# A four-layer convolution network: smaller pieces for the stores of the attention scores

## Chip, cores and metric

The kernel runs on one core of a Trainium2 chip. The metric is the time of one execution on the device in microseconds (us); the number for a kernel is the median of several executions. The profile is one more execution, recorded by the hardware profiler.

## What is computed

The input `x` has the shape (4, 256, 64, 64) in f32. Four layers follow each other, each of the form `x = x + layer(groupnorm(x))`. The change lies in layer 0, an axial attention over the columns of the image with 16 groups of channels:

```python
qkv = bn(einsum('nci,oc->noi', xp, w_qkv))         # n = 4*64, 64 positions i
q, k, v = split(qkv)                               # 16 groups, 8 + 8 + 16 channels
qe = einsum('ngci,cij->ngij', q, q_emb)
ke = einsum('ngci,cij->ngij', k, k_emb)
qk = einsum('ngki,ngkj->ngij', qe, ke)             # the scores
sim = softmax(bn(concat([qk, qe, ke])).sum(1))
attn, attn_e = einsum(sim, v), einsum(sim, v_emb)
```

The batch norm of `qk`, `qe` and `ke` needs sums over the whole batch, so all scores are computed and put away before the first softmax. Layers 1 to 3 are 3x3 convolutions with ternary, binary and generated weights.

## The kernel before

Layer 0 has three stages. The first normalises the input, projects it to q, k and v, and writes q and k to the scratch tensors `q_d[b]` in DRAM. The second computes the scores `qk`, writes them to `qk_d[b]` (one tensor for each of the 4 batch items, shape 8 x 128 x 4096), and gathers the sums for the batch norm; beside this it prepares the weights of the later layers. The third (`from_scores`) reads the scores back, forms the softmax and multiplies with the values. Then come the convolutions.

The second stage is a loop over 4 batch items `b` and 8 pairs of groups `gp`, 32 steps in all (L634, L635). A step has four beats, over `nb` and `jh` (L642, L645). In each beat:

- `projections` (L457) has SyncE load a piece of q and k for a later step, 128 KB with 64 rows of 2 KB (L463), pinned to its place in the program (L468). The data are needed two values of `j`, that is four steps, later.
- `position_terms` (L495) runs 64 small matmuls into PSUM (L505), and VectorE moves the result to SBUF in two transposes (L512).
- `finish(last, k)` (L612) calls `product` (L517) for the step before: 64 matmuls (L526), two ScalarE evictions into the tile `o` (L532) and a sum of squares (L538). So the tile `o` of a step is filled in the four beats of the next step.
- `finish` then issues one store out of the list `whole` (L616 to L625). A tile is put on `whole` after its fourth product, so its four stores are written in the beats of the step after that. Each store is pinned by `keep_in_program_order`.
- One slice of the weight preparation, mostly on VectorE, runs until the generator `weights` is used up.

The tile `o` (L640) has 128 partitions of 4096 f32 (16 KB), with two buffers. The first store of a tile needs all four products, so SyncE waits for ScalarE there; the other three have nothing new to wait for. The second buffer is free again when the four stores have landed, and is written by the first product of the step after next.

DRAM row `2 j + r` of `qk_d[b][gp]` belongs to partition `64 r + j`. A store before takes the partitions of one `r` and one half of the columns: 64 rows of 8 KB, 512 KB. The scores of the last step are stored after the loop in two pieces of 1 MB (L660), which the change leaves alone.

All loads and stores that matter here go through SyncE's queue, in program order: the loads of L463, the stores, at the end of the stage the loads of the tables `rw`, `ve` and `cnt` of the third stage (L771 to L779), the last scores (L660), the values `vb` (L820) and the scores `si` (L855). The tile framework gives every DMA of SyncE's and ScalarE's queues one of eight semaphores in turn, and a DMA waits until the one that had its semaphore before has landed. The POOL queue carries the prepared weights (L567, L596) and the loads of the raw ones (L574, L578).

Of the kernel before, what the change touches and what calls it, by code (L numbers as in the profile page):

```python
# [21 lines left out]
HW = 4096  # L22
# [19 lines left out]
def network(ctx: ExitStack, tc, x, wqkv, relm, relt, relw, relv, counts, masks, vecs, rowv, ab, w1, l2w1, l2w2, l3w, mats, out):  # L42
# [4 lines left out]
    nc = tc.nc  # L47
# [5 lines left out]
    def scratch(name, shape):  # L53
        return dram.tile(shape, F32, name=name, tag=name)
# [4 lines left out]
    qk_d = [scratch(f"qk_d{b}", [GP, P, HW]) for b in range(B)]  # L59
# [106 lines left out]
    with ExitStack() as ph:  # L166
# [112 lines left out]
        for b in range(B):  # L279
            xs, gm, rs = ready  # L280
            qs = [qp.tile([P, 8, 8, 64], F32, name=f"qs{t}_{b}", tag="qs") for t in range(2)]
            for k in range(NB):
# [37 lines left out]
                if k % 2 == 1:  # L320
                    for r in range(2):
                        nc.scalar.dma_start(
                            out=vt_d[b][k // 2, r].rearrange("p a c m -> p a (c m)"),
                            in_=vs.rearrange("p (a r c) m -> p r a (c m)", r=2, c=16)[:, r],
# [7 lines left out]
                if k in (3, 7) and 2 * b + k // 4 - 1 in range(len(pieces)):  # L332
                    i = 2 * b + k // 4 - 1
# [3 lines left out]
            for t in range(2):  # L337
                for l in range(8):
                    nc.sync.dma_start(
                        out=q_d[b][:, l, t].rearrange("a r c f -> (r c) a f"),  # L340
                        in_=qs[t][:, EIGHT[l]].rearrange("p a h -> p (a h)"),
# [36 lines left out]
        for t in range(2):  # L378
            for l in range(8):
                nc.gpsimd.dma_start(  # L380
                    out=qs_d[t, l].rearrange("r c a f -> (r c) a f"), in_=qtot[:, t, EIGHT[l]]
# [28 lines left out]
    with ExitStack() as ph:  # L410
# [106 lines left out]
        def product(units, o, k, col, gp, name):  # L517

            ps = [psq.tile([P, 8, 64], F32, name=f"pq_{name}_{k}_{nb}", tag="pq") for nb in range(2)]
            for m in range(8):  # L520
                n = 8 * k + m
                for nb, ts in enumerate(units):
                    for g in range(2):
                        src = 64 * (g ^ nb)
                        rows = slice(src, src + 64)
                        nc.tensor.matmul(  # L526
                            ps[nb][64 * g : 64 * g + 64, m, :], lhsT=ts[1][rows, n // 2, :, n % 2],
                            rhs=ts[0][rows, n // 2, :, n % 2], start=True, stop=True, tile_position=(src, 64 * g),
                        )
            for nb in range(2):  # L530
                n = 32 * nb + 8 * k
                nc.scalar.activation(  # L532
                    o[:, :, n : n + 8, :], ps[nb].rearrange("p n (a b) -> p a n b", b=2), AF.Copy,
                    accum_out=acc[:, nb, gp, col : col + 1],
                )
            part = o.rearrange("p a (x n) b -> p a x (n b)", x=2)[:, :, :, 16 * k : 16 * k + 16]
            junk = jp.tile([P, 32, 2, 16], BF16, name=f"sq_{name}_{k}", tag="sq", bufs=1)
            nc.scalar.activation(junk, part, AF.Square, accum_out=acc[:, 2, gp, col : col + 1])  # L538
# [73 lines left out]
        def finish(step, k):  # L612
            units, o, b, gp = step
            product(units, o, k, 4 * b + k, gp, f"{b}_{gp}")

            if whole:  # L616
                wb, wgp, wo, part = whole[0]
                store = nc.sync.dma_start(
                    out=qk_d[wb][wgp].rearrange("(j r) f -> r j f", r=2)[part % 2][:, bass.ts(part // 2, HW // 2)],
                    in_=wo[bass.ts(part % 2, 64), bass.ts(part // 2, 16)].rearrange("p a n b -> p (a n b)"),  # L620
                )
                tc.keep_in_program_order(store)
                whole[0] = (wb, wgp, wo, part + 1)
                if part == 3:
                    whole.pop()  # L625
            if k == 3:
                whole.append((b, gp, o, 0))
# [6 lines left out]
        for b in range(B):  # L634
            for gp in range(GP):  # L635
                j = 4 * b + gp // 2
                if j == 2 and gp % 2 == 0:
                    load_sums()
                q = qs[j]
                o = op.tile([P, 32, 64, 2], F32, name=f"o_{b}_{gp}", tag="o")  # L640
                units = []
                for nb in range(2):  # L642
                    ts = [tp_.tile([P, 16, 64, 2], F32, name=f"t{t}_{b}_{gp}_{nb}", tag=f"t{t}") for t in range(2)]
                    units.append(ts)
                    for jh in range(2):  # L645
                        if j + 2 < 4 * B:
                            projections(j + 2, 4 * (gp % 2) + 2 * nb + jh)
                        position_terms(q, ts, gp, nb, jh, f"{b}_{gp}_{nb}")
                        if last is not None:
                            finish(last, 2 * nb + jh)  # L650
                        if j > 0:
                            next(weights, None)
                last = (units, o, b, gp)
                term_sums(j, q, gp % 2)
                if gp % 2 == 0 and j + 1 < 4 * B:
                    scaled(j + 1, qs[j + 1])
        for k in range(4):
            finish(last, k)
        for r in range(2):
            nc.sync.dma_start(  # L660
                out=qk_d[B - 1][GP - 1].rearrange("(j r) f -> r j f", r=2)[r],
                in_=o[bass.ts(r, 64)].rearrange("p a n b -> p (a n b)"),
# [80 lines left out]
    def from_scores(general, keep):  # L743
# [373 lines left out]
        X_PLACES = [(0, 1, 2, 3), (4, 5, 0, 2), (1, 3, 4, 0), (5, 2, 1, 4)]  # L1117

        def conv_layer(name, ph, weights, layout, own, load, biases, first, finish):


# [768 lines left out]
```

## Time and profile before

| | us |
|---|---|
| median of 3 runs (2811.41 to 2813.65) | 2812.06 |
| the profiled execution | 2810.18 |
| its span, first to last instruction | 2808.3 |
| TensorE busy in the span | 2416.8 (86%) |
| VectorE busy | 1980.8 (71%) |
| ScalarE busy | 1204.5 (43%) |
| SyncE's DMA queue (q1): 195232 packets, 359.5 MB, share of the 16 DMA engines | 42.3% |

In a profile line, L12 is line 12 of the kernel. Engines are PE (TensorE matmul), PEld (TensorE weight load, beside PE), DVE (VectorE), ACT (ScalarE), POOL (GpSimd) and SPq (SyncE's queue, where a row is the issuing of a DMA, not its transfer). In a wait, `<-` names what ended it; "issue" is time in which an engine waited for nothing that the profile shows. The second stage lies at about 300 to 946 us of the span. 31 of its 32 tiles `o` are stored by L618, 124 stores; the 30 steps between the first stores of neighbouring tiles last 16.9 to 23.9 us, 19.7 us in the mean.

### The profile page before, as it was taken

Reading aid. Unit: us, or ns where it says so; the run is one execution under the profiler, and the core shown is the slowest. Engines: PE = TensorE matmul, PEld = TensorE weight load, DVE = VectorE, ACT = ScalarE, POOL = GpSimd, SP = SyncE. Lnnn points to the kernel's source line nnn. Section 1 sums busy time; section 2 is a strip of 40 time slices with the busy share of each in tenths; the row PEclk is TensorE's granted clock in tenths of the full one; section 3 lists DMA queues with packets and bytes.
Section 4 is the critical chain, followed back from the end, with each engine's and each line's share of the span. In section 5 each row is a group of like instructions: output and inputs, shape, how many; then the busy total and the mean of one; then the engine's idle time right before and its main releaser. Section 6 shows DMA issues by size and latency. Waiting matters only on the chain.

```text
span 2808.3 us, 77698 instructions
## 1 busy us (share of the span) xinstructions
PE 2416.8 (86%) x34632; PEld 1583.8 (56%) x34632; DVE 1980.8 (71%) x3362; ACT 1204.5 (43%) x1984; POOL 105.4 (4%) x201
## 2 busy tenths in 40 slices
PE   7999888888887778888874899998988859999998
PEld 4666555555555566667663677776555424444443
DVE  6665788878665455566657878986888877958642
ACT  4555355545444654454443564653448521110100
POOL 0000100000000100000000000000000000000000
PEclk9999899989999798989986899999999979999999
DMA  6867375657545777777766456534336752324101
GB/s 240 270 188 212 81 198 144 165 146 186 143 124 148 218 251 246 253 244 252 253 228 226 163 171 202 172 120 179 125 121 247 283 189 91 120 105 150 45 33 44
DMA packets 258233, 489.81 MB, mean 174 GB/s; under 512 B 26785, under 2 KB 143137, under 8 KB 237153
## 3 DMA queue, kind: packets, MB, share of 16 engines
q1 hardware_dynamic: 195232, 359.50, 42.3%
q0 software_dynamic: 14400, 66.53, 6.1%
q10 hardware_dynamic: 48256, 58.73, 6.1%
q8 instruction: 273, 4.47, 0.6%
q14 instruction: 72, 0.58, 0.1%
HBM read 281.46 MB, written 203.23 MB: 173 GB/s over the span
## 4 chain that ended last, share of the span: by engine, by line
issue 23%; PE 18%; DMA 10%; DVE 10%; ACT 5%; POOL 0%; SPq 0%; ACTq 0%; DVEq 0%; POOLq 0%
PE dc L1356 8%; DMA at_d<-o_False 3%; PE e_False L866 2%; DMA x<-x_d 2%; PE pr_False L935 2%; PE pc L1450 2%; DVE pt L876 2%; PE pe_False L969 2%; PE den_False L917 2%; DMA dx<-in_x 1%; DMA qc_False<-q_d 1%; ACT pt L906 1%; DVE e_tr L1439 1%; DMA z_d<-dx 1%; PE pa_False L944 1%
## 5 line engine op out<-in xcount | busy, mean ns | idle before, releaser
L1065 PE MATMUL gc<-gtr,g_u 128*128 128x512 f32 x1152 | 504.5, 600 | 11.1 <-DVE gtr L1043 6.7
L512 DVE STREAM_TRANSPOSE t<-pd 128x1024 f32<-128x1024 f32 x256 | 304.7, 1228 | 136.7 <-PE pd L505 131.9
L1065 PEld LDWEIGHTS gc<-gtr,g_u 128*128 128x128 f32 x1152 | 219.6, 191 | 287.6 <-issue 270.2
L505 PE MATMUL pd<-rm,qb 64*32 64x256 f32 x8192 | 322.6, 406 | 59.7 <-DVE t L512 30.3
L532 ACT ACTIVATE o<-pq 128x512 f32<-128x512 f32 x256 | 150.6, 594 | 311.6 <-PE pq L526 311.6
L1450 PE MATMUL pc<-e_tr,e_k 128*64 128x512 bf16 x2304 | 265.4, 391 | 18.3 <-DVE e_tr L1439 11.8
L1356 PE MATMUL dc<-dh,d_u 128*128 128x512 f32 x768 | 235.0, 416 | 35.8 <-ACT dh L1333 35.8
L505 PEld LDWEIGHTS pd<-rm,qb 64*32 64x32 f32 x8192 | 174.5, 112 | 160.1 <-issue 65.1
L906 ACT ACTIVATE pt<-pt,sm 128x512 f32<-128x512 f32 x256 | 162.6, 709 | 173.9 <-DVE pt L876 173.9
L1356 PE MATMUL dc<-dl,d_u 128*128 128x512 f32 x768 | 229.9, 409 | 0.3
L1450 PEld LDWEIGHTS <-e_k 128*64 128x64 bf16 x2304 | 146.7, 112 | 133.9 <-issue 26.9
L526 PEld LDWEIGHTS pq<-t,t 64*64 64x64 f32 x8192 | 146.3, 139 | 100.7 <-issue 89.1
L526 PE MATMUL pq<-t,t 64*64 64x64 f32 x8192 | 168.4, 227 | 40.1 <-issue 35.6
L1356 PEld LDWEIGHTS dc<-dh,d_u 128*128 128x128 f32 x768 | 149.5, 196 | 77.1 <-ACT dh L1333 37.7
L876 DVE TENSOR_TENSOR pt<-e_False,si_False 128x1024 f32<-128x1024 f32 x128 | 151.4, 1215 | 30.6 <-PE e_False L866 30.3
L1356 PEld LDWEIGHTS dc<-dl,d_u 128*128 128x128 f32 x768 | 146.4, 192 | 42.1 <-DVE dl L1334 3.6
L1083 ACT COPY gc_c<-gc 128x512 f32<-128x512 f32 x32 | 18.6, 581 | 344.8 <-PE gc L1065 344.8
L866 PE MATMUL e_False<-qc_False,rw 32*128 32x256 f32 x1024 | 129.7, 474 | 25.5 <-DVE pt L876 12.5
L538 ACT ACTIVATE sq<-o 128x1024 bf16<-128x1024 f32 x128 | 135.3, 1057 | 4.0
L293 PE MATMUL po<-xg,wt 128*128 128x512 f32 x256 | 120.2, 608 | 5.3 <-DVE st L300 3.7
L969 PE MATMUL pe_False<-pt,ve 128*32 128x64 f32 x4096 | 90.3, 243 | 35.6 <-issue 28.7
L308 PE MATMUL pv<-wt,xg 128*128 128x256 f32 x512 | 120.6, 384 | 0.0
(403 smaller groups left out, 3596.0 us busy)
## 6 DMA issues: line engine op xcount, KB each, us to landing
si_False<-qk_d SPq DMA_DIRECT2D x64, 1024.0 KB
qk_d<-o SPq DMA_DIRECT2D x124, 512.0 KB
x<-x_d SPq DMA_DIRECT2D x32, 1056.0 KB
xa<-in_x SPq DMA_DIRECT2D x16, 1024.0 KB
vt_d<-vs ACTq DMA_DIRECT2D x32, 512.0 KB
q_d<-qs SPq DMA_DIRECT2D x64, 256.0 KB
qb<-q_d SPq DMA_DIRECT2D x128, 128.0 KB
qc_False<-q_d SPq DMA_DIRECT2D x64, 256.0 KB
```

Of the source, the lines that this page charges most:

```text
L505: nc.tensor.matmul(pds[t][32 * c : 32 * c + 32, m].rearrange("p j k -> p (j k)"), lhsT=q[rows, 2 * (gp % 2) + g, a, 32 * nb : 32 * nb + 32 ...
L512: nc.vector.transpose(ts[t][:, :, 32 * jh : 32 * jh + 32].rearrange("p a j b -> p j a b"), pds[t].rearrange("p m j k -> p j m k"),)
L526: nc.tensor.matmul(ps[nb][64 * g : 64 * g + 64, m, :], lhsT=ts[1][rows, n // 2, :, n % 2], rhs=ts[0][rows, n // 2, :, n % 2], start=True, ...
L532: nc.scalar.activation(o[:, :, n : n + 8, :], ps[nb].rearrange("p n (a b) -> p a n b", b=2), AF.Copy, accum_out=acc[:, nb, gp, col : col + 1],
L538: nc.scalar.activation(junk, part, AF.Square, accum_out=acc[:, 2, gp, col : col + 1])
L866: nc.tensor.matmul(es[x_ // 2][:, x_ % 2, :, :, par], lhsT=rw[rows, 63 - i : 127 - i].rearrange("p j r -> p (j r)"), rhs=q[rows, :, par, k ...
L876: nc.vector.tensor_tensor(dst, e, src, ALU.add)
L906: nc.scalar.activation(s, s, AF.Exp, scale=s2q[:, gp : gp + 1])
L969: nc.tensor.matmul(ps[32 * a : 32 * a + 32, m // 2, :, m % 2], lhsT=ve[:, 63 - i, :], rhs=pt[:, i // 2, a, :, i % 2], start=True, stop=Tru ...
L1065: nc.tensor.matmul(ms[k], lhsT=u[t][:, dx, k, bass.ts(co, P)], rhs=vs[t][:, k, :, dx : dx + 64], start=(first and dx == 0), stop=(last and ...
L1356: nc.tensor.matmul(at[k], lhsT=u[t][:, dx, k, bass.ts(co, P)], rhs=v[:, k, :, dx : dx + 64], start=(first and p_ == 0 and dx == 0), stop=( ...
L1450: nc.tensor.matmul(m[64 * g : 64 * g + 64], lhsT=parts[:, g, i, k, dx, :], rhs=vs[g][:, k, 8 * (q % 2) : 8 * (q % 2) + 8, dx : dx + 64], s ...
```

## The change

Each store of 512 KB becomes four of 128 KB. In beat `part` (0 to 3) the pieces `i = 4 part` to `4 part + 3` are issued one behind the other: pieces with even `i` take partitions 0 to 63, those with odd `i` take 64 to 127, and `i // 2` picks one of eight column blocks of 512 f32. So a row of a piece is 2 KB, and a beat now stores a quarter of the columns of all 128 partitions, where it stored half the columns of half of them. A tile has 16 stores in place of 4, with the same bytes to the same places.

```diff
             if whole:
                 wb, wgp, wo, part = whole[0]
-                store = nc.sync.dma_start(
-                    out=qk_d[wb][wgp].rearrange("(j r) f -> r j f", r=2)[part % 2][:, bass.ts(part // 2, HW // 2)],
-                    in_=wo[bass.ts(part % 2, 64), bass.ts(part // 2, 16)].rearrange("p a n b -> p (a n b)"),
-                )
-                tc.keep_in_program_order(store)
+                for i in range(4 * part, 4 * part + 4):
+                    store = nc.sync.dma_start(
+                        out=qk_d[wb][wgp].rearrange("(j r) f -> r j f", r=2)[i % 2][:, bass.ts(i // 2, 512)],
+                        in_=wo[bass.ts(i % 2, 64), bass.ts(i // 2, 4)].rearrange("p a n b -> p (a n b)"),
+                    )
+                    tc.keep_in_program_order(store)
                 whole[0] = (wb, wgp, wo, part + 1)
                 if part == 3:
                     whole.pop()
```

## The prediction, on record before the result

> **What bounds the kernel now.** I read the page first, then the timeline of SyncE's queue in the second stage, then the waits there, and last the DMA share in and between the bursts of stores. The timeline shows two tiles of scores:
>
> ```profile
> 613.10 0.46 SPq L618 DMA_DIRECT2D qk_d<-o  x1
> 613.61 0.63 SPq L463 DMA_DIRECT2D qb<-q_d  x1
> 614.29 1.86 SPq L618 DMA_DIRECT2D qk_d<-o  x1
> 616.20 0.62 SPq L463 DMA_DIRECT2D qb<-q_d  x1
> 616.86 2.10 SPq L618 DMA_DIRECT2D qk_d<-o  x1
> 619.00 0.63 SPq L463 DMA_DIRECT2D qb<-q_d  x1
> 619.97 1.75 SPq L618 DMA_DIRECT2D qk_d<-o  x1
> 621.77 0.64 SPq L463 DMA_DIRECT2D qb<-q_d  x1
> 630.68 0.47 SPq L618 DMA_DIRECT2D qk_d<-o  x1
> ```
>
> The stores are written one to a beat, but they run as a burst: the first waits for the finished tile, the other three and the four loads between them follow at once. SyncE is busy from 613.1 to 622.4, 9.3 us, and idle until 630.7. The first store takes 0.46 us to issue, the later ones about 1.9 us: these are held back by the transfers ahead of them, not by the issuing. The waits say the same; columns are sum, count and longest, the first row from the queue's own waits, the others from the stage:
>
> ```profile
> SPq L618 <- ACT o L532: 337.1, 31, 28.4
> ...
> ACT o L532 <- PE pq L526: 284.2, 126, 6.3
> ...
> DVE t L512 <- PE pd L505: 128.7, 77, 6.7
> ...
> PE pq L526 <- issue: 35.0, 27, 3.6
> PE pd L505 <- DVE t L512: 28.8, 23, 2.2
> ...
> PE pd L505 <- issue: 26.9, 24, 2.8
> PE pq L526 <- ACT o L532: 4.3, 3, 2.9
> ```
>
> SyncE waits 337 us for tiles. ScalarE and VectorE wait for matmuls, TensorE for VectorE and for its own issue. In the whole stage no row has ScalarE waiting for a store to free its buffer, nor VectorE or TensorE for a load of q and k. TensorE, busy 83% to 86% in each window of 100 us, with VectorE at 62% to 84%, sets the pace. The stores are off the path. How far off, the next ScalarE rows and the DMA share tell (the windows are one burst and the rest of its step):
>
> ```profile
> 634.41 0.60 ACT L532 ACTIVATE o<-pq 128x512 f32<-128x512 f32 x1 [2.57 <-PE pq L526]
> ...
> 613.10:625.60 12.50, 11.08 (x397) 7.49 (x403) 12.26 (x23) 6.22 (x15) 0.56 (x1) 1.00 0.84 232
> 625.60:630.68 5.08, 4.39 (x134) 3.38 (x119) 3.15 (x4) 3.83 (x12) 0.53 (x1) 1.00 0.35 135
> ```
>
> The last two columns are the busy share of the 16 DMA engines and GB/s. The transfers of the burst end about 12.5 us after it starts. The buffer that they free is first written at 634.41, 21.3 us after the burst started. That leaves about 8 us of slack in each step.
>
> **What the Trainium skill says.** "SBUF — State Buffer", section "Door 1: The DMA port swizzle", says that the bandwidth depends on how many of 16 ports the partitions reach, and that partitions 0 to 63 and 64 to 127 lie on different ports; half the partitions reach half of them. The trace agrees: the 8 KB packets of L618, each from 64 partitions, take 613 ns in the median and 309 ns at best, which is 214 and 424 GB/s over 16 engines. "DMA: Bandwidth & Descriptors", section "Why small descriptors are slow", gives a packet a fixed overhead of about 3 cycles beside its 32-byte beats: estimated from that, 67 cycles for the 64 beats of 2 KB, some 5% over. In the trace 2 KB packets take 84 ns, four of them 336 ns against 309 ns for 8 KB: 9% more. The same page's "Rules for kernel authors" asks for 1 MiB per DMA at best. The trace has no such loss for back-to-back 128 KB pieces when little else runs, as the loads below show.
>
> **The change part by part.** The compiled order of all five engines is the same in both kernels; only SyncE has 372 more stores (124 x 3). The work per tile:
>
> *Issue on SyncE.* The nearest row is L463, the same 128 KB in 64 rows of 2 KB, here as a long run early in the kernel (min, median, max ns):
>
> ```profile
> L463 SPq DMA_DIRECT2D qb<-q_d x22: 574/575/836, 104.2 to 123.8; - x22
> ...
> L618 SPq DMA_DIRECT2D qk_d<-o x124: 445/1876/2904, 329.0 to 923.3; - x124
> ```
>
> Eleven of those loads follow each other at 0.62 us. The unhindered store has a simpler pattern and takes 0.45 us, so 0.50 with the gap. Sixteen stores cost 8.0 to 9.9 us, four loads 4 x 0.67 = 2.7 us: 10.7 to 12.6 us for a burst, against 9.3 us. The growth of 1.4 to 3.3 us lies in SyncE's idle time, which is 337 / 31 = 10.9 us per tile. If that cover were gone, all of it would count 30 times.
>
> *Transfer.* The bytes are equal. At the halved rate 128 KB take 0.61 us, so 16 take 9.8 us as before; at full rate 16 x 0.34 = 5.4 us. Neighbouring pieces now lie on opposite halves of the ports, so engines that drift apart can use both: the value may fall below the present one, hardly rise by more than the 9%, 0.9 us. I take the upper end: last data at about 12.5 + 0.9 = 13.4 us, and 1.7 us for a landing (the page's figure for the 4 KB stores `qs_d`). 15.1 us against 21.3 us: no wait for the buffer. Gain or loss: 0.
>
> *Semaphores.* A DMA waits for the eighth before it. Eight small ones at 0.50 to 0.62 us reach back 4.0 to 5.0 us. That covers a 128 KB store and its landing, 0.6 + 1.7 us. A backlog would make SyncE wait for the transfers, as it does now at issue. Queued behind are only loads needed four steps (79 us) later.
>
> *ScalarE.* The first L532 of a step waits for the stores' semaphores, eight in place of four, so 120 more waits over 30 steps. At 38 ns for a semaphore row on ACT, and two waits to a row, this is at most 60 x 38 ns = 2.3 us. It runs while ScalarE waits for its matmul (284 us in the stage), so I take 0; the ends are 0 and +2.3 us.
>
> *Other queues.* Shorter packets let others in sooner. The one visible victim is a weight load of 144 KB or more on POOL (L574), for which ScalarE waited 6.9 us at 603 and TensorE then 3 us. Its four 4.6 KB packets per engine need 0.7 us alone and took 2.8 us beside 8 KB ones; with 2 KB ones I estimate 4 x (0.18 + 0.16) = 1.4 us. Ends: -1.4 and 0. I take 0, since the next matmul wait would take up part of it.
>
> *End of the stage.* The last burst starts at 920.2 and its data run out at about 930.5. L660 starts at 933.4, when ScalarE is done. Issue of 16 without loads ends at 928.2 to 930.1. Slack 3 us; cost 0. The tables of L771 to L779 start after a burst too and are needed from 947.
>
> The sum on the profiled execution is 2810.2 + 0 = 2810.2 us. That execution lay 1.9 us under the median, so the median stays 2812. With the bounds, -1.4 to +2.3, and the spread of the runs shown, the likeliest case spans 2809 to 2816.
>
> **The rivals.** *Finer packets speed TensorE's supply.* TensorE loses 62 us to "issue" in the stage. The 16 KB instruction packets share the DMA engines with the stores, and if they queue behind 8 KB packets, shorter ones help. Summed over the 30 bursts of 12.5 us, the waits of TensorE on issue are 40.7 of 375 us, 10.9%; in the rest of the steps 24.2 of 216 us, 11.2%. The instruction packets take 0.96 us in the median in both. So the bursts are not what delays TensorE. Were 30% of the 40.7 us saved all the same: 2800.
>
> *SyncE becomes the clock (the slower side).* If each store cost 1.2 us, SyncE would need 16 x 1.2 + 2.7 = 21.9 us for a step of 19.7 us, +2.2 us x 30 = +66 us: 2878. For it: 256 KB stores with 2 KB rows went out at 1.3 us each beside ScalarE's stores:
>
> ```profile
> 84.37 9.16 SPq L339 DMA_DIRECT2D q_d<-qs  x7
> ```
>
> Against it: these carry twice the bytes and packets, and the first of that run went out at 0.64 us each. It decides from (19.7 - 2.7) / 16 = 1.06 us per store on, also the point where the buffer comes too late (16 x 1.06 + 2.7 + 1.7 = 21.4).
>
> *Only the end of the stage slips.* At over 0.82 us per store the last burst ends after 933.4; at 1.2 us it ends at 939.4 and moves L660, the values and the next scores by 6 us: 2818.
>
> **How the numbers follow.** A measurement of this kernel can tell about 0.2%, 5.6 us, from no change. Likeliest, nothing moves: 0.79, 2812 us. Finer packets help: 0.08. SyncE's clock: 0.06. The end slips: 0.07. So faster 0.08, same 0.79, slower 0.13. The range takes in the likeliest case, the bounds and the slipped end, and leaves out 2800 and 2878: 2804 to 2820.
>
> **What would show it.** Right: the stores issue at 0.45 to 0.65 us, bursts last 11 to 13 us, SyncE's wait for L532 falls to some 240 to 295 us, the steps still last 19.7 us, no ScalarE wait on a store appears, TensorE's issue waits stay near 62 us. Wrong: ScalarE L532 waiting for a DMA `qk_d<-o` (SyncE's clock), L660 well after 934 (the end), or issue waits well under 62 us (finer packets).

## The result and the profile after

The changed kernel takes 2774.33 us in the median (2766.54 to 2777.9, 4 runs) against 2811.73 us on the same chip: the ratio is 0.9853, with a 95% interval of 0.9824 to 0.9882. It is faster by some 37 us, where no change was forecast. Its profiled execution took 2766.54 us with a span of 2764.8 us.

The time comes from the second stage alone. From its first matmul of L505 to its last of L526 it took 637.8 us before and 591.9 us after; from there to TensorE's last matmul it took 1863.3 and 1864.3 us. The mean step fell from 19.7 to 18.3 us. In all profiles of the changed kernel the lines behind the diff are one higher, and the store is L619.

SyncE's queue, two tiles of scores (start, duration, row):

```profile
596.85 2.39 SPq L619 DMA_DIRECT2D qk_d<-o  x4
599.28 0.63 SPq L463 DMA_DIRECT2D qb<-q_d  x1
599.95 3.14 SPq L619 DMA_DIRECT2D qk_d<-o  x4
603.14 0.63 SPq L463 DMA_DIRECT2D qb<-q_d  x1
603.81 2.39 SPq L619 DMA_DIRECT2D qk_d<-o  x4
606.25 0.63 SPq L463 DMA_DIRECT2D qb<-q_d  x1
606.92 2.69 SPq L619 DMA_DIRECT2D qk_d<-o  x4
609.65 0.63 SPq L463 DMA_DIRECT2D qb<-q_d  x1
614.80 2.39 SPq L619 DMA_DIRECT2D qk_d<-o  x4
```

Four stores cost 2.4 to 3.1 us, and the next tile is due 18.0 us after this one. The same stores by their durations (min, median, max ns):

```profile
L619 SPq DMA_DIRECT2D qk_d<-o x496: 445/596/2310, 328.3 to 889.8; - x166
```

SyncE's own waits:

```profile
SPq L619 <- ACT o L532: 116.7, 29, 26.4
```

The waits of the other engines from 320 to 930 us:

```profile
ACT o L532 <- PE pq L526: 240.6, 121, 5.1
...
DVE t L512 <- PE pd L505: 79.8, 68, 5.7
...
PE pd L505 <- DVE t L512: 30.1, 27, 2.3
...
PE pq L526 <- issue: 23.5, 26, 2.6
...
PE pd L505 <- issue: 6.7, 11, 1.6
```

TensorE's two waits on issue fell from 35.0 + 26.9 to 23.5 + 6.7 us: 31.7 us less. The page has a second fall, in the busy time of its matmuls. First before, then after:

```profile
L505 PE MATMUL pd<-rm,qb 64*32 64x256 f32 x8192 | 322.6, 406 | 59.7 <-DVE t L512 30.3
```

```profile
L505 PE MATMUL pd<-rm,qb 64*32 64x256 f32 x8192 | 305.5, 389 | 41.4 <-DVE t L512 32.3
```

The same 8192 matmuls are 17.1 us shorter, 389 in place of 406 ns each. The clock did most of that: from 320 us on, one that begins at half clock takes 625 ns in the mean before and 612 after, any other 381 and 380 ns, and fewer begin at half clock. The small matmuls of L526 hardly changed (227 and 225 ns). The next rows are 565 us of the stage, before and after; ahead of the last two columns stands the granted clock:

```profile
320.00:885.00 565.00, 477.86 (x15050) 327.44 (x15050) 429.55 (x689) 288.43 (x722) 10.41 (x17) 0.95 0.59 153
```

```profile
320.00:885.00 565.00, 496.96 (x16060) 346.99 (x16058) 448.95 (x722) 311.49 (x779) 15.81 (x20) 0.98 0.63 164
```

In the trace's clock records TensorE ran at half rate for 58.0 us of the stage before and 27.3 us after (from the first store to the last matmul of L526), in pieces of 3.4 us and multiples. At most half of the saved 30.7 us is won, 15.4 us. TensorE started 18.3 matmuls per us at half rate and 27.2 at the full one, a third fewer, which makes it 10 us. By this estimate the sum is 31.7 us and 10 to 15 us, 42 to 47 us, against the stage's 45.9 us.

What TensorE waits for when it "waits for nothing" can be found in the packet records. Its instructions come as packets of 16 KB (queue q8), one for each 4 to 5 us of the stage. I took its standstills of over 0.4 us, from the first store to 40 us before the end of the stage, and asked which ended 1.0 to 1.6 us after the end of such a packet. Before, 39 of 63 did, 53.6 of 85.8 us. As one packet comes each 4 to 5 us, chance would put about one in seven there.

A count settles what they are. The trace of the kernel before has 69534 records of TensorE's instructions and 273 of these packets, so a packet brings some 255, and 256 if one takes 64 bytes. 38 of the 39 standstills end at the same place in the count: TensorE has then started 193 instructions more than a multiple of 256. Of the other 24 only one ends there. So TensorE has used up one packet and stands until the next has come: these are standstills for want of instructions. After, they are 31.2 us, 24 of 32 at that place. Sorted by the time since the first store of the tile was issued, they take this share of the time in the first 30 steps:

```
us from the first store     0-2 2-4 4-6 6-8 8-10 10-12 12-14 14-16 16-18 18-20
before (%)                    0   1   4  13   17    34    12    10     8     0
after (%)                     1   2   8   6    4    14     8    15     1     4
```

Before, they stand in and just behind the stores' transfers: nearly none in the first 4 us, none after 18 us. After, the bursts are longer and fill most of the step.

### The profile page after: what moved, and what is told of

The parts are those of the page before. It is cut to its first block, busy times and chain, and to the rows that moved or that the text cites. A ratio compares the mean times of both kernels' runs of the same rounds, so it can differ in the third digit from the quotient of the medians.

```text
span 2764.8 us, 78125 instructions
## 1 busy us (share of the span) xinstructions
PE 2398.3 (87%) x34632; PEld 1576.4 (57%) x34632; DVE 1980.3 (72%) x3362; ACT 1205.8 (44%) x1984; POOL 105.4 (4%) x201
## 4 chain that ended last, share of the span: by engine, by line
issue 38%; PE 30%; DVE 14%; DMA 11%; ACT 5%; POOL 1%; SPq 1%; DVEq 0%; ACTq 0%; POOLq 0%
PE pd L505 5%; PE dc L1357 4%; PE po L293 3%; PE pv L308 3%; PE pq L526 3%; DMA at_d<-o_False 2%; PE e_False L867 2%; DMA x<-x_d 2%; PE pr_False L936 2%; DVE pt L877 2%; PE pe_False L970 2%; DMA dx<-in_x 2%; PE den_False L918 2%; PE pa_False L945 2%; PE pc L1451 2%
## 5 line engine op out<-in xcount | busy, mean ns | idle before, releaser
L505 PE MATMUL pd<-rm,qb 64*32 64x256 f32 x8192 | 305.5, 389 | 41.4 <-DVE t L512 32.3
L1451 PE MATMUL pc<-e_tr,e_k 128*64 128x512 bf16 x2304 | 265.3, 391 | 20.5 <-DVE e_tr L1440 13.3
L505 PEld LDWEIGHTS pd<-rm,qb 64*32 64x32 f32 x8192 | 168.4, 108 | 134.7 <-DVE t L512 57.4
L526 PEld LDWEIGHTS pq<-t,t 64*64 64x64 f32 x8192 | 146.0, 138 | 86.1 <-issue 71.6
L526 PE MATMUL pq<-t,t 64*64 64x64 f32 x8192 | 168.5, 225 | 28.6 <-issue 23.5
```

Source lines behind the costliest of these rows:

```text
L505: nc.tensor.matmul(pds[t][32 * c : 32 * c + 32, m].rearrange("p j k -> p (j k)"), lhsT=q[rows, 2 * (gp % 2) + g, a, 32 * nb : 32 * nb + 32 ...
L526: nc.tensor.matmul(ps[nb][64 * g : 64 * g + 64, m, :], lhsT=ts[1][rows, n // 2, :, n % 2], rhs=ts[0][rows, n // 2, :, n % 2], start=True, ...
L1451: nc.tensor.matmul(m[64 * g : 64 * g + 64], lhsT=parts[:, g, i, k, dx, :], rhs=vs[g][:, k, 8 * (q % 2) : 8 * (q % 2) + 8, dx : dx + 64], s ...
```

## The experiments

In all of them the kernel before is changed as shown, unless another start is named. In all but `small_8k` and `small_64`, the compiled order of TensorE, VectorE and ScalarE is that of the kernel before, and SyncE has the same other DMAs. "Want of instructions" below is the sum of the standstills just described, in the one profiled execution of a run.

**big_2k: rows alone.** Each store of 512 KB takes every other block of 512 columns.

```diff
-  out=...[part % 2][:, bass.ts(part // 2, HW // 2)],
-  in_=wo[bass.ts(part % 2, 64), bass.ts(part // 2, 16)].rearrange("p a n b -> p (a n b)"),
+  out=...[part % 2].rearrange("j (c y f) -> j y c f", y=2, f=512)[:, part // 2],
+  in_=wo[bass.ts(part % 2, 64)].rearrange("p a n b -> p (a n b)")
+      .rearrange("p (c y f) -> p y c f", y=2, f=512)[:, part // 2],
```

> Four stores of 512 KB a tile as before, but each takes every other block of 512 columns, so its rows are 2 KB (256 of them). The first theory: TensorE's instruction packets share the DMA engines with the stores and wait behind 8 KB packets, so the packet length alone brings the gain; it expects about 2774 us and TensorE's issue waits in the second stage near 30 us (before: 62 us). The second theory: small stores keep less in the queue and are paced by SyncE; it expects about 2812 us and 62 us. The third theory, the two halves of the ports in turn within a beat: 2812 us.

Measured: 2809.41 us, ratio 1.0002 (0.9976 to 1.0028); want of instructions 54.6 us. The trace has 2 KB packets. TensorE's waits on issue from 320 to 885 us, against 53.5 us before and 30.2 us in the changed kernel in that window:

```profile
PE pq L526 <- issue: 30.6, 27, 4.0
PE pd L505 <- issue: 25.3, 22, 2.4
```

My first theory, that the row length counts, falls.

**big_1k: shorter rows still.** The same with `f=256`.

> As the 512 KB stores with 2 KB rows, with rows of 1 KB (512 of them). If the wait behind a store's packet is in proportion to its length, three quarters of it went from 8 KB to 2 KB (38 us), and another eighth goes here: about 2768 us. If a floor is reached at 2 KB: 2774 us. Pacing: 2812 us.

Measured: 2816.25 us, 1.0035 (1.0011 to 1.0059); want of instructions 64.3 us. At 512 KB a store, rows of 8, 2 and 1 KB are alike or slightly worse.

**small_2k_half: the halves not in turn.** As the changed kernel, but a beat's four pieces lie in one half of the partitions.

```diff
+  for i in range(4):
+      store = nc.sync.dma_start(
+          out=...[part % 2][:, bass.ts(4 * (part // 2) + i, 512)],
+          in_=wo[bass.ts(part % 2, 64), bass.ts(4 * (part // 2) + i, 4)]...
```

> Sixteen stores of 128 KB with rows of 2 KB as in the changed kernel, but the four of a beat take one half of the partitions and half of the columns, as the stores before did. The packet length theory expects 2774 us, as does pacing. If it is the halves in turn that count, 2812 us.

Measured: 2771.15 us, 0.9866 (0.9826 to 0.9905); want of instructions 26.3 us. The waits on issue, in the same window:

```profile
PE pq L526 <- issue: 20.3, 20, 3.4
PE pd L505 <- issue: 5.3, 10, 1.6
```

The whole gain is there without the alternation, so the ports are not its cause.

**small_8k: small stores, long rows.** 16 rows of 8 KB, every fourth partition.

```diff
+  for i in range(4):
+      out=qk_d[wb][wgp].rearrange("(j s r) f -> r s j f", r=2, s=4)[part % 2][i][:, bass.ts(part // 2, HW // 2)],
+      in_=wo[64 * (part % 2) + i : 64 * (part % 2) + 64 : 4, bass.ts(part // 2, 16)]...
```

> Sixteen stores of 128 KB a tile, four in a beat, but with rows of 8 KB: 16 rows, every fourth partition of one half. The packet length theory expects about 2812 us and issue waits near 62 us. The pacing theory (small stores): 2774 us and 30 us. The halves in turn: 2812 us, since all four stores of a beat lie in one half.

Measured: 2951.58 us, 1.0508 (1.0469 to 1.0547). It doesn't answer the question: with these stores the scheduler put the products of TensorE and ScalarE in another order, and TensorE now waits for ScalarE, 65 times:

```profile
PE pq L526 <- ACT o L532: 46.5, 65, 0.8
```

Only one standstill ends at the place in the count where a packet is used up, but with a stage of 755 us in place of 638 TensorE also asks for packets more slowly, so that says little. Small stores with rows of 8 KB stay untried in the same order.

These runs left two theories. Either a DMA engine serves a store's whole part, 1/16 of the DMA, before it turns to the instruction packet in another queue; or small stores are issued more slowly and leave the engines freer.

**mid_256: 256 KB.** Two stores in a beat with rows of 4 KB.

```diff
+  for i in range(2):
+      out=...[part % 2][:, bass.ts(2 * (part // 2) + i, 1024)],
+      in_=wo[bass.ts(part % 2, 64), bass.ts(2 * (part // 2) + i, 8)]...
```

> Eight stores of 256 KB a tile, two in a beat, 64 rows of 4 KB. Since 512 KB stores with 2 KB rows gained nothing, the row length is out. Two theories are left. Share theory: a DMA engine hands each store its whole part (1/16 of the DMA) before it turns to the instruction packets in another queue, so the part's bytes count: 32 KB before, 8 KB in the changed kernel, 16 KB here; about 2786 us expected (two thirds of the gain, if the wait is in proportion). Pace theory: small stores cost SyncE more issue time, the engines are less busy in a burst and instruction packets find them free; eight issues a tile stretch the burst little, so about 2800 us.

Measured: 2783.39 us, 0.9906 (0.9870 to 0.9942); want of instructions 39.4 us.

**big_1m: 1 MB.** One store in every second beat.

```diff
+  if part % 2 == 1:
+      out=...[part // 2],
+      in_=wo[bass.ts(part // 2, 64)].rearrange("p a n b -> p (a n b)"),
```

> Two stores of 1 MB a tile, 64 rows of 16 KB, in the second and the fourth beat. Share theory: the part of a store is 64 KB, twice that of before, so TensorE starves longer: 2840 us or more. Pace theory: the burst is as dense as before, about 2809 us.

Measured: 2874.17 us, 1.0228 (1.0191 to 1.0266); want of instructions 95.1 us. TensorE's waits, 320 to 885 us:

```profile
PE pd L505 <- issue: 43.7, 21, 3.6
PE pq L526 <- issue: 38.9, 26, 5.0
```

That is 82.6 us, against 53.5 us before and 30.2 us in the changed kernel in the same window; over the whole of its longer stage, to 993 us, it is 109.4 us. From 6 to 10 us after the first store TensorE lacks instructions for 37% to 40% of the time, where before it was 13% to 17%.

**rb_512: pace alone.** The old stores, with a pause in the middle of a burst.

```diff
+  if part == 1:
+      back = nc.sync.dma_start(out=seen, in_=qk_d[wb][wgp][1:2, 2032:2048])
+      tc.keep_in_program_order(back)
```

> Stores of 512 KB with 8 KB rows as before, but after the second of a tile SyncE loads 64 bytes of what it wrote, and so waits until it has landed. This thins the burst out (8 us of issue becomes some 12 to 14 us) and leaves each store's size alone. Pace theory: most of the gain, about 2780 us. Share theory: about 2809 us.

Measured: 2812.45 us, 1.0010 (0.9979 to 1.0040); want of instructions 63.9 us. The pause is there, 7.8 us from the second store to the load that waits for it, and SyncE needs 12.3 us in the mean for a burst with its four loads, in place of 9.4 us:

```profile
609.44 0.47 SPq L619 DMA_DIRECT2D qk_d<-o  x1
609.95 0.62 SPq L463 DMA_DIRECT2D qb<-q_d  x1
610.63 1.87 SPq L619 DMA_DIRECT2D qk_d<-o  x1
618.43 0.22 SPq L625 DMA_DIRECT2D seen<-qk_d  x1
```

The pause gains nothing. But on both sides of it the stores are as dense as before: from 2 to 6 us after the first store the 16 DMA engines are busy for 96% of the time, as before. So this run tests a pause, not a looser stream. The better test of pace is `mid_256`: from 2 to 8 us its engines are busy for 94% of the time, before for 97%, and its want of instructions is lower all the same. In the changed kernel they are busy for 71%, so from 256 to 128 KB a looser stream may have its part.

**small_64: 64 KB.** Eight stores in a beat with rows of 1 KB, `range(8)` and 256 columns. ScalarE's compiled order differs here, TensorE's in 13 rows.

> Thirty-two stores of 64 KB a tile, eight in a beat, 64 rows of 1 KB. SyncE needs at least 32 x 0.50 + 2.7 = 18.7 us for a step that lasts 18.3 us in the changed kernel. Share theory (4 KB parts): TensorE starves less, but SyncE becomes the clock, 2775 to 2800 us. Pace theory: likewise. The run is to show where SyncE's issue takes over, and whether TensorE's waits after instruction packets go on falling.

Measured: 3018.35 us, 1.0731 (1.0692 to 1.0769), far slower than either theory said. SyncE issues without a pause and needs about 26 us for a tile, and ScalarE waits for the buffer (320 to 1100 us):

```profile
ACT o L532 <- DMA qk_d<-o: 365.7, 29, 17.4
ACT o L532 <- PE pq L526: 107.8, 91, 2.6
```

A burst with its four loads lasts 26.3 us in the mean, so a store costs (26.3 - 2.7) / 32 = 0.74 us, not the 0.50 us of an unhindered one. Want of instructions is 5.1 us, but with TensorE slowed by so much, that says nothing on the parts.

**after_again, si_only, si_256: the same in another stage.** The changed kernel once more; then the loads of scores of the third stage in four pieces, in the kernel before and in the changed one.

```diff
-  nc.sync.dma_start(
-      out=si.rearrange("p a i f -> p a (i f)"),
-      in_=qk_d[b][4 * th : 4 * th + 4].rearrange("a p f -> p a f")[:, :, bass.ts(k, 512)],
-  )
+  for a in range(4):
+      nc.sync.dma_start(
+          out=si[:, a].rearrange("p i f -> p (i f)"), in_=qk_d[b][4 * th + a][:, bass.ts(k, 512)]
+      )
```

> The changed kernel once more, beside the next two on the same chip: about 0.986 of the kernel before, 2772 us.

> The kernel before, with its stores of 512 KB, but in the third stage each load of scores of 1 MB (64 KB for each DMA engine) is four of 256 KB (16 KB each), with the same rows of 2 KB. In that stage TensorE stands still for 52 us right after instruction packets. Share theory: about a third to a half of it goes, 17 to 26 us: 2783 to 2792 us. If the second stage's stores are a case of their own: 2809 us. If SyncE's extra 192 issues of 0.36 us each delay the scores, slower than 2809 us.

> Both together: the stores of 128 KB of the changed kernel and the loads of scores of 256 KB. Share theory: the two gains add, since they lie in different stages: 2745 to 2757 us, the fastest of all. Otherwise about 2772 us or slower.

Measured: `after_again` 2772.50 us, 0.9875 (0.9847 to 0.9903). `si_only` 2804.21 us, 0.9972 (0.9947 to 0.9997): about 8 us faster, at most half of what was forecast. `si_256` 2751.89 us, 0.9821 (0.9784 to 0.9858): the fastest median of all. Its interval overlaps that of `after_again`, and its profiled third stage lasted 559.6 us against 560.6 us there. Want of instructions from 890 to 1460 us went from 53.3 to 37.4 us in the changed kernel, but only from 52.3 to 48.1 us in the kernel before. `big_2k`, whose third stage is that of the kernel before, had 35.1 us there, so one execution can't tell such a difference. That the loads of the third stage cost TensorE instructions too is not shown.

The four sizes in one view, by the bytes that each of the 16 DMA engines gets of one store. The two waits are of instruction packets: the mean time from TensorE's first instruction past the place named above, where a packet is used up, to the start of the next packet, once for the places that TensorE reaches in the first 8 us from the first store of a tile, once for those that it reaches after 12 us. The last row is half the time of a part, from its packets' median:

```
part per engine             8 KB     16 KB    32 KB    64 KB
time (us)                   2774     2783     2809     2874
want (us)                   31       39       54       95
wait, first 8 us (us)       1.19     1.90     2.58     3.95
wait, after 12 us (us)      1.39     1.21     1.20     1.13
half a part (us)            0.24     0.59     1.23     2.54
```

With 16, 32 and 64 KB the early packets wait 0.69, 1.38 and 2.82 us longer than the late ones, close to half a part each time: what a packet would lose on average that comes at any moment of a part and has to let it end. With 8 KB there is no such excess, but the burst there goes on past 12 us. Over the whole stage the wait is 1.90 us before, 1.85 and 1.94 us with rows of 2 and 1 KB (`big_2k`, `big_1k`), 1.94 us with the pause (`rb_512`), and 1.34, 1.36 and 1.39 us with the small stores (changed kernel, `after_again`, `small_2k_half`), in one profiled execution each. So it goes with the size of the DMA, not with its rows.

## Why the prediction was wrong

**What was right.** The stores cost the other engines almost nothing directly. SyncE took the 496 stores into its idle time, at 0.60 us in the median. ScalarE waited for a store once, 2.1 us at 879 us of the span, and for the weight load of L574 6.4 us, where it had been 6.9. The last scores (L661 now) started 2.2 us after ScalarE had finished the tile, straight behind the last small store, and before at once; yet from the last matmul of L526 to the first of the third stage it took 15.3 us after and 15.5 us before. The extra semaphore waits on ScalarE cost nothing that shows. The place of the danger from SyncE was right too: past its limit ScalarE waits for `qk_d<-o`, as `small_64` shows. The issue was underpriced: a burst with its four loads lasts 15.1 us on average, not 10.7 to 12.6, since (15.1 - 2.7) / 16 = 0.78 us go to a store where I had 0.50 to 0.62. SyncE's wait fell to 117 us, not to 240 to 295.

**Two of its readings don't stand.** The 613 ns of the 8 KB packets were taken to show that half the partitions give half the rate. But the loads of L463 reach 64 partitions too, and their 2 KB packets took 84 ns, 390 GB/s over 16 engines; what made the 8 KB packets slow is not shown. And those loads at 0.62 us for 128 KB are 211 GB/s, half of the 424 GB/s of the best packets, so they are no proof that pieces of 128 KB lose nothing. Neither decided the forecast.

**The step that failed is the rival "finer packets speed TensorE's supply".** The sum had no term for TensorE's supply; it put its change at nothing. The rival named the right victim and was set aside at 0.08 for two reasons that don't hold.

First, the comparison of issue waits, 10.9% inside the bursts and 11.2% outside. It counted every wait on issue and cut at 12.5 us. An instruction packet that is late does not stop TensorE at once. It stops some microseconds later, when the instructions in hand run out: by the count it had up to 268 in hand when a packet began, 150 in the median, at some 53 started per us. So a late packet from a burst is booked in part behind it. Sorted by time since the first store, and only those that end with an instruction packet, the standstills are nearly absent in the first 4 us, fill 13% to 34% from 6 to 12 us, and are absent after 18 us. 16.0 of their 58.9 us in the 30 steps lie behind the cut.

Second, the time of the instruction packets, 0.96 us in and out of the bursts. This is how long a packet runs once it has begun. It even grew, to 1.15 us in the changed kernel. What fell is the wait ahead of it, from 1.90 to 1.34 us in the mean by the count above; in the first 8 us of a burst from 2.58 to 1.19 us.

**The price of that rival was wrong as well.** It allowed 30% of 40.7 us, 12 us. The issue waits fell by 31.7 us, and the half clock by 30.7 us, by the estimate above worth another 10 to 15 us, for which the prediction had no term. The Trainium skill has it, in "TensorE: Matmul & The Clock Gate", section "Part 1: The HAM clock gate": TensorE drops to half its clock after an idle window of about 3.4 us. The trace agrees with the length of the pieces, but not with a wholly idle window: in the 3.4 us ahead of each of the 15 falls of the stage before, TensorE was busy for 22% to 59% of the time. That fewer standstills bring fewer slow windows fits the profiled executions at the ends (20.5 us at half clock for `small_2k_half`, 118.0 for `big_1m`), not the order of those between: `big_1k`, with 64.3 us of want, had only 30.7 us.

**And its mechanism was wrong.** It blamed the length of a row. At 512 KB a store, rows of 2 and 1 KB gain nothing; with 256 and 128 KB stores the gain comes, and with 1 MB the loss. What counts is the size of the DMA. I read it thus: an engine serves its whole part of a store before it turns to the queue with the instructions. The Trainium skill leaves room for this in "DMA: Bandwidth & Descriptors", section "Queues, rings and completion order": an engine takes turns between queues only when a packet is done, and a packet holds several descriptors, typically about 9 to 17 and at most 64. It doesn't say that a packet is the whole part. In the stores of 512 KB a part is 4 rows of 8 KB, 16 of 2 KB or 32 of 1 KB, all under the bound if a row is a descriptor. I had taken a row, which is what the trace records as a packet, for what an engine serves in one turn. The part's time fits: 4 rows of 613 ns are 2.5 us, 4 rows of 2 KB at 120 ns 0.5 us, and the waits in the view of the four sizes grow by half a part. The turn itself is inferred: no record shows an instruction packet in a queue.

What stays open: 31 us of want remain at 8 KB parts, and small stores with rows of 8 KB, which would part the bytes of a DMA from its rows from the other side, weren't tried in the same order. Along the four sizes the rows grew too, from 2 to 16 KB; at 512 KB they changed nothing. The number of DMAs changed with their size in every run, and was not varied alone.

**The range** of 2804 to 2820 us rested on three runs within 2.2 us of each other. The later runs of the kernel before lie between 2790 and 2836 us, so 0.2% was no measure of its noise; yet the miss of 30 us below the range is not noise.

## What to carry to other kernels

When TensorE waits for "issue" in short gaps, look whether the gaps end a fixed time after an instruction packet, and at the same place in the count of instructions; then the DMAs beside it delay its instructions, and their size matters even if no engine ever waits for them. Splitting large DMAs helps (here down to 128 KB), until the issuing queue becomes the clock: price an issue as it runs under load (0.7 to 0.8 us here), not alone (0.45 us), and keep the burst inside the step. Shortening the rows inside a DMA of the same size did nothing.

## What had not been expected of the hardware

TensorE resumed 1.0 to 1.6 us after the end of an instruction packet in 39 of 63 standstills, 38 of them at the same place in the count of its instructions. Stores for which no engine waited in the kernel before cost it 1.5%, and with twice the size of a store another 2.3%. A fifth to a third of the gain, by estimate, was the clock: 58.0 us at half rate became 27.3 us, and TensorE need not be idle for a whole window of 3.4 us to lose it.
